# An adaLN block with a gated scan and an FP4 feed-forward: the first stage's opening rewritten, with the input projection's weights laid out by input features

## The chip, the cores and the metric

The kernel runs on one core of a Trainium2 chip. The metric is the device time of one execution in microseconds. TensorE (PE in the profile) multiplies matrices, VectorE (DVE), ScalarE (ACT) and GpSimd (POOL) work elementwise, and SyncE (SP) issues most DMAs. [...]

## The reference, cut to what matters

The input x has 2 sequences of 4096 tokens with 512 features. Six modulation rows per sequence come from a small matrix product. Then follow two residual branches: a gated linear recurrence, and a feed-forward network whose operands are rounded to a 4-bit grid in blocks of 16.

```python
mod = (silu(c) @ wmod).reshape(2, 6, 1, -1)
sa, ca, ga, sb, cb, gb = (mod[:, n] for n in range(6))
ga, gb = floor_of_size(ga, 0.25), floor_of_size(gb, 0.25)      # sign kept
h = layernorm(x) * (1 + ca) + sa
xn = h / norm(h) * sqrt(512) * gamma
q, kv, a = split(xn @ W_qkva.T, 3)
y = scan(y_t = sigmoid(a_t) * y_(t-1) + kv_t)
x = x + ga * (q * y)
h = layernorm(x) * (1 + cb) + sb
x = x + gb * fp4_linear(silu(fp4_linear(h, w_gate)) * fp4_linear(h, w_up), w_down)
```

## The kernel before, in words

The kernel has two stages, each under an order written out by hand: the order of the program is the order in every engine's queue.

**Stage A** computes the recurrence and, beside it, quantizes the feed-forward weights. It goes over 16 blocks of 512 tokens and, in each, over 4 groups `e` of 128 output features: 64 slots. In a slot `mix` (from line 394 on, matmul at L407) makes three products (a, kv, q) of 128 features by 512 tokens, 12 matmuls each. Every operand is split into a high and a low f16 half, and three passes (high-high, high-low, low-high) over 4 pieces of 128 input features make the 12. In the first slot alone the matmuls are cut into pieces of 128 tokens, so that each can start when its 128 tokens have come. Six PSUM banks take the products, three for even and three for odd slots. `gates` (ScalarE sigmoid, L419), `scan` (VectorE, L425) and `read_out` (L434) follow; `halves` (L441) splits the result for a transpose by DMA (L443), `joined` (L449) puts it back together, and `residual` adds it to x on GpSimd (L457) and stores it (L459).

The tokens of a later block are prepared tile by tile (128 tokens): load (L350), moments (L153, L158), reciprocal deviation on GpSimd (L160, L161), `center` and `shift` on VectorE (L166, L172), square sum (L368), gain (L373, L375), high half (L381), low half (L386), and a DMA transpose into `xT` (L390). In the loop each slot prepares one tile, for the block after the current one.

W_qkva stands in memory by output features. So in the **opening** each of its 12 pieces of 128 x 512 is loaded (L208), multiplied with gamma along its columns (L295), squared and summed along its row (L299), scaled by a reciprocal row norm (L302, L303), cut into halves (L322 or L324, and L330) and transposed by DMA into `wqT` (L338). The three gains per group (L310, L313) put the norm back later. `start()` gives this for three of the groups; the fourth is worked off in the first two slots of the loop.

The modulation: `mod_spread` (L221) multiplies the scale and shift rows into all 128 partitions at once for the first sequence (ca, sa); `mod_rows` (L238) makes two rows for both sequences, which `mod_store` (L277) sends to memory for later; `mod_columns` (L252) makes the gate ga by columns in the first slot.

SP issues the loads and the transposes in one queue. A DMA waits until the eighth one before it in that queue has landed.

**Stage B** begins after slot 63, at L902: for each of 64 tiles of 128 tokens the gate and up products (L902), the quantization of the hidden row, and the down product (L949). The change does not touch it.

Of the kernel before, what the change touches and what calls it, by code (L numbers as in the profile page):

```python
# [6 lines left out]

# [10 lines left out]
P = 128  # L18
# [25 lines left out]
def tile_adaln_block(  # L44
# [106 lines left out]
    def moments(xt):  # L151
        st = small.tile([P, 6], F32, name="st", tag="st")
        V.bn_stats(st, xt)  # L153
        return st

    def mean_rstd(st):
        mv = small.tile([P, 2], F32, name="mv", tag="mv", bufs=5)
        V.bn_aggr(mv, st)  # L158
        rstd = small.tile([P, 1], F32, name="rstd", tag="rstd", bufs=5)
        G.tensor_scalar(rstd, mv[:, 1:2], 1e-5, None, ALU.add)  # L160
        G.tensor_tensor(rstd, rstd, mhalf[:, 0:1], ALU.pow)  # L161
        return mv[:, 0:1], rstd
# [32 lines left out]
    wq = {divmod(n, 3): piece(2, n, 1) if n < 11 else piece(1, 2 * KC, 1) for n in range(12)}  # L195
# [3 lines left out]
    with nc.allow_non_contiguous_dma(reason="c is 4 KB"):  # L199
        for b in range(B):  # L200
            S.dma_start(cT[:, :, b], c[b].rearrange("(k p) -> p k", p=P))
    warm = atile([P, 4], F32, "warm")
    A.activation(warm, mhalf, AF.Sigmoid)
    A.activation(sc, cT, AF.Sigmoid)
    V.tensor_mul(sc, sc, cT)

    def load_part(e, part):
        S.dma_start(wq[e, part], w_qkva[part * D + e * P : part * D + (e + 1) * P, :])  # L208

    def load_mod(s, pieces=1):  # L210
        w = KC // pieces
        for k in range(0, KC, w):
            S.dma_start(
                wm[s][:, k : k + w, :],
                wmod[k * P : (k + w) * P, s * D : (s + 1) * D].rearrange("(k p) e -> p k e", p=P),
            )

    def mod_spread(s, b):
        pm = side((P, D))
        for k in range(KC):  # L220
            T.matmul(  # L221
                pm,
                sc[:, k, b : b + 1].to_broadcast([P, P]),
                wm[s][:, k, :],
                start=k == 0,
                stop=k == KC - 1,
            )
        return pm

    def mod_rows(*mods, one_by_one=False):  # L230

        pm = side((P, D))
        rows = [(s, slice(32 * n, 32 * n + B)) for n, s in enumerate(mods)]
        steps = [(k, *r) for k in range(KC) for r in rows]
        if one_by_one:
            steps = [(k, *r) for r in rows for k in range(KC)]
        for k, s, at in steps:
            T.matmul(  # L238
                pm[at, :],
                sc[:, k, :],  # L240
                wm[s][:, k, :],
                start=k == 0,
                stop=k == KC - 1,
                tile_position=(0, at.start),
            )
        return pm, rows

    def mod_columns(s):
        pm = side((P, KC, B))
        for e in range(KC):  # L250
            for k in range(KC):
                T.matmul(  # L252
                    pm[:, e, :],
                    wm[s][:, k, e * P : (e + 1) * P],
                    sc[:, k, :],
                    start=k == 0,
                    stop=k == KC - 1,
                )
        return pm

# [7 lines left out]

    def mod_store(pm, rows):
        row = apool.tile([P, D], F32, name="row", tag="row", bufs=1)  # L270
        for s, at in rows:
            if s == 5:
                mag = apool.tile([P, D], F32, name="mag", tag="y", bufs=3)
                signed_floor(row[at, :], pm[at, :], mag[at, :])
            else:
                A.activation(row[at, :], pm[at, :], AF.Copy, bias=1.0 if s in (1, 4) else 0.0)
            G.dma_start(modd[s], row[at, :])  # L277
# [6 lines left out]
    gam = ctile([P, D], F32, "gam", tag="mod_gb")  # L284
    wqT = atile([P, 2 * KC, 3 * D], F16, "wqT")
    us = atile([P, KC, 3], F32, "us")
    rs = atile([P, KC, 3], F32, "rs")
    gq = atile([P, KC, B], F32, "gq")

    def load_qkva(e):  # L290
        for part in (2, 1, 0):
            load_part(e, part)

    def gamma_qkva(e, part, engine=G):
        engine.tensor_tensor(wq[e, part], wq[e, part], gam, ALU.mult)  # L295

    def square_qkva(e, part):
        sq = work.tile([P, D], BF16, name="sq", tag="sq", bufs=1)
        A.activation(sq, wq[e, part], AF.Square, accum_out=us[:, e, part : part + 1])  # L299

    def inverse_qkva(e, a=0, b=3):
        V.tensor_scalar(rs[:, e, a:b], us[:, e, a:b], 1e-36, 2.0**-28, ALU.max, ALU.mult)  # L302
        G.tensor_tensor(rs[:, e, a:b], rs[:, e, a:b], mhalf[:, : b - a], ALU.pow)  # L303

    def scale_qkva(e):
        inverse_qkva(e)
        gain_qkva(e)

    def gain_qkva(e):
        V.tensor_scalar(  # L310
            us[:, e, :], us[:, e, :], 1e-36, 2.0**-28 / (XGAIN * XGAIN), ALU.max, ALU.mult
        )
        G.tensor_tensor(us[:, e, :], us[:, e, :], phalf[:, :3], ALU.pow)  # L313

    whl = {}

    def hi_qkva(e, part, on_act):
        w = wq[e, part]
        hl = whl[e, part] = new_hl()
        rsc = rs[:, e, part : part + 1]  # L320
        if on_act:
            A.activation(hl[:, 0, :], w, AF.Copy, scale=rsc)  # L322
        else:
            V.tensor_scalar(hl[:, 0, :], w, rsc, None, ALU.mult)  # L324

    def lo_qkva(e, part):
        w = wq[e, part]
        hl = whl.pop((e, part))
        r = part * KC + e
        V.scalar_tensor_tensor(  # L330
            out=hl[:, 1, :],
            in0=w,
            scalar=rs[:, e, part : part + 1],
            in1=hl[:, 0, :],
            op0=ALU.mult,
            op1=ALU.subtract,
        )
        S.dma_start_transpose(wqT[:, :, r * P : (r + 1) * P], flat(hl))  # L338
# [15 lines left out]

    def norm_stats(g):
        xstat[g] = mean_rstd(xstat[g])
# [7 lines left out]
    def norm_square(g):  # L364
        h = xh[g]
        sq = work.tile([P, D], BF16, name="sq", tag="sq", bufs=1)
        ss = small.tile([P, 1], F32, name="ss", tag="ss")
# [3 lines left out]
    def norm_gain(g, engine=V):  # L371
        h, ss = xh[g]
        engine.tensor_scalar(ss, ss, 1e-24, 1.0 / (D * XGAIN * XGAIN), ALU.max, ALU.mult)  # L373
        rn = small.tile([P, 1], F32, name="rn", tag="rn")
# [9 lines left out]
    def norm_lo(g, xT):  # L384
        h, rn, hl = xh.pop(g)
        V.scalar_tensor_tensor(  # L386
            out=hl[:, 1, :], in0=h, scalar=rn, in1=hl[:, 0, :], op0=ALU.mult, op1=ALU.subtract
        )
        t = g % KC
        S.dma_start_transpose(xT[:, :, t * P : (t + 1) * P], flat(hl))  # L390
# [7 lines left out]
    def mix(i, xT, e):  # L398
        ps = [bank(3 * (e % 2) + j) for j in range(3)]
        width = P if i == 0 and e == 0 else TB  # L400
        for t in range(0, TB, width):
            for pp, part in zip(ps, PARTS):
                r = part * KC + e
                n = 0
                for k in range(KC):
                    for wp, xp in PASSES:
                        T.matmul(  # L407
                            pp[:, t : t + width],
                            wqT[:, wp * KC + k, r * P : (r + 1) * P],
# [5 lines left out]
        return i, e, ps  # L415
# [6 lines left out]
    def scan(i, e, ps, sig):  # L422
        y = apool.tile([P, TB], F32, name="y", tag="y", bufs=3)
        init = 0.0 if i % BPB == 0 else carry[e]
        V.tensor_tensor_scan(out=y, data0=sig, data1=ps[1], initial=init, op0=ALU.mult, op1=ALU.add)  # L425
        if i % BPB != BPB - 1:
# [3 lines left out]
        return i, e, ps, y  # L430
# [8 lines left out]
    def halves(i, e, y):  # L439
        yh = apool.tile([P, 2, TB], U16, name="yh", tag="yh", bufs=1)  # L440
        A.copy(yh, y.bitcast(U16).rearrange("p (t h) -> p h t", h=2))  # L441
        yt = apool.tile([P, 2, KC, P], U16, name="yt", tag="yt", bufs=2)
# [12 lines left out]
    def residual(i, e, y):  # L455
        xs = xrows[i][:, :, e * P : (e + 1) * P]
        G.tensor_tensor(xs, xs, y.rearrange("p (t e) -> p t e", t=KC), ALU.add)  # L457
        b, t0 = divmod(i * TB, N)
# [136 lines left out]
    def stats_x(x1):  # L595
# [7 lines left out]
        rstd = small.tile([P, 1], F32, name="rstd", tag="rstd", bufs=5)  # L603
# [57 lines left out]
    def start():  # L661
        a, b_, c_ = PARTS

        def load_mod_piece(s, k):
            S.dma_start(wm[s][:, k, :], wmod[k * P : (k + 1) * P, s * D : (s + 1) * D])

        load_mod(1, KC)
        norm_load(0)
        S.dma_start(gam, gamma.partition_broadcast(P))
        for k, then in enumerate((PARTS[0], PARTS[1], PARTS[2], None)):  # L670
            if then is None:
                norm_load(1)
            else:
                load_part(0, then)
            load_mod_piece(0, k)
        norm_load(2)
        norm_load(3)
        load_qkva(1)
        norm_load(KC)
        pc = mod_spread(1, 0)  # L680
        ps = mod_spread(0, 0)
        pair = mod_rows(1, 0, one_by_one=True)

        norm_moments(0)
        norm_stats(0)
        gamma_qkva(0, a, V)
        A.activation(ca[0], pc, AF.Copy, bias=1.0)
        square_qkva(0, a)
        gamma_qkva(0, b_, V)
        square_qkva(0, b_)  # L690
        inverse_qkva(0, a, a + 1)
        norm_center(0)
        gamma_qkva(0, c_, V)
        inverse_qkva(0, b_, b_ + 1)
        hi_qkva(0, a, True)
        square_qkva(0, c_)
        lo_qkva(0, a)
        inverse_qkva(0, c_, c_ + 1)
        hi_qkva(0, b_, True)
        norm_moments(1)  # L700
        norm_stats(1)
        lo_qkva(0, b_)
        A.copy(sa[0], ps)
        norm_center(1)
        hi_qkva(0, c_, True)
        norm_shift(0)
        norm_square(0)
        lo_qkva(0, c_)
# [366 lines left out]
```

## Time and profile before

| | us |
|---|---|
| median of 3 runs | 1926.46 |
| lowest, highest | 1925.21, 1926.94 |
| the profiled execution | 1928.68 |
| its span, first to last instruction | 1926.9 |
| first matmul of the mix, block 0 | 25.68 |
| first matmul of block 1 (slot 4) | 77.70 |
| first matmul of stage B | 551.11 |

The span of a profile is what lies between the first and the last instruction; the execution's own time has 1.8 us more. The profile names an instruction by the line that issues it, so a helper that several steps call has one line. "Idle before" in a timeline is the time in which the engine had nothing to run, and after the arrow stands what ended it. PEclk is the share of the full TensorE clock that was granted.

### The profile page before, as it was taken

The numbers are of one execution on the slowest core, as the hardware profiler recorded it, in microseconds if no ns is written. First come the engines' busy times: TensorE is split into PE (matmuls) and PEld (weight loads), VectorE is DVE, ScalarE is ACT, GpSimd is POOL, SyncE is SP. The second block draws the span as 40 slices with busy tenths as digits, with TensorE's granted clock in tenths as the row PEclk, the third lists the DMA queues.
The fourth block names the chain that finished last, engine by engine and source line by source line (L and its number), as shares of the span: only waits on it lengthen the run. The fifth ranks groups of instructions, "written<-read, shape, count | busy, mean of one in ns | idle before, by whom it ended". The sixth has DMA issues, their size and how long they took to land.

```text
span 1926.9 us, 25653 instructions
## 1 busy us (share of the span) xinstructions
PE 1897.6 (98%) x9220; PEld 898.6 (47%) x9220; DVE 1604.6 (83%) x2677; ACT 997.3 (52%) x1705; POOL 413.7 (21%) x597
## 2 busy tenths in 40 slices
PE   7899999999999999999999999999999999999998
PEld 4344444444444444444444444444444444444444
DVE  6778889999869988888888888878888888888865
ACT  4555567777755544544454444444444444444432
POOL 4545566566421100000000000001000000000000
PEclk9999999999999999999999999999999999999999
DMA  9797788998733344334433443344334334433333
GB/s 232 174 261 180 177 192 201 224 200 197 170 83 71 76 84 74 64 66 81 75 63 67 80 74 74 68 79 80 63 70 80 72 63 71 81 70 63 64 67 58
DMA packets 483201, 206.67 MB, mean 107 GB/s; under 512 B 439622, under 2 KB 440902, under 8 KB 483072
## 3 DMA queue, kind: packets, MB, share of 16 engines
q1 hardware_dynamic: 468624, 171.50, 41.7%
q0 software_dynamic: 14448, 33.52, 9.6%
q8 instruction: 72, 1.18, 0.3%
q14 instruction: 57, 0.47, 0.1%
HBM read 63.12 MB, written 33.58 MB: 50 GB/s over the span
## 4 chain that ended last, share of the span: by engine, by line
PE 92%; DVE 3%; DMA 1%; ACT 1%; issue 1%; POOL 1%; SPq 0%; ACTq 0%; POOLq 0%; DVEq 0%
PE mm L902 46%; PE sd L949 24%; PE mm L407 22%; DMA scratch<-in_L_attn_W_qkva_dram 1%; DMA xT<-hl 1%; DVE hl L330 0%; POOL xr L457 0%; DVE y L434 0%; DVE ld L172 0%; POOL rs L303 0%; ACT sq L299 0%; DVE xn L122 0%; PE sd L238 0%; ACT yh L441 0%; DVE hl L324 0%
## 5 line engine op out<-in xcount | busy, mean ns | idle before, releaser
L902 PEld LDWEIGHTS <-x2T 128*128 128x128 f16 x4608 | 450.9, 98 | 470.6 <-issue 2.5
L407 PE MATMUL mm<-xT,wqT 128*128 128x512 f16 (+1 forms) x2412 | 506.1, 373 | 15.6 <-DMA xT<-hl 11.3
L902 PE MATMUL mm<-wuT,x2T 128*128 128x512 f16 (+1 forms) x2304 | 487.7, 361 | 2.2 <-DVE hid L922 2.2
L902 PE MATMUL mm<-wgT,x2T 128*128 128x512 f16 (+1 forms) x2304 | 487.7, 361 | 0.0
L949 PE MATMUL sd<-wdT,hT 128*128 128x512 f16 x2112 | 465.8, 379 | 0.0
L407 PEld LDWEIGHTS <-wqT 128*128 128x128 f16 x2412 | 232.4, 99 | 290.1 <-issue 21.6
L949 PEld LDWEIGHTS <-hT 128*128 128x128 f16 x2112 | 206.7, 98 | 242.6
L917 ACT ACTIVATE silu<-mm,u 128x512 f32<-128x512 f32 (+1 forms) x192 | 125.1, 652 | 285.9 <-PE mm L902 282.1
L922 DVE SCALAR_TENSOR_TENSOR hid<-mm,u,silu 128x512 f32<-128x512 f32 (+1 forms) x192 | 128.4, 672 | 140.9 <-PE mm L902 130.7
L604 POOL TENSOR_SCALAR rstd<-vs 128x1 f32<-128x1 f32 x64 | 14.5, 226 | 990.5 <-ACT sq L602 990.5
L143 ACT ACTIVATE u<-ud,rms 128x1 f32<-128x1 f32 x64 | 19.0, 297 | 277.9 <-DVE rms L139 277.9
L120 ACT ACTIVATE sle<-sl 128x512 f16<-128x512 f32 (+2 forms) x162 | 147.2, 909 | 0.0
L113 ACT ACTIVATE she<-sh 128x1408 bf16<-128x1408 bf16 (+1 forms) x128 | 128.5, 1004 | 4.0
L441 ACT COPY yh<-y 128x1024 uint16<-128x1024 uint16 x64 | 67.0, 1047 | 94.7 <-DVE y L434 80.6
L973 POOL DMA_DIRECT2D out_dram<-o x63 | 56.2, 893 | 269.8 <-DVE o L967 266.0
L122 DVE SCALAR_TENSOR_TENSOR xn<-hid,xn 128x1408 f32<-128x1408 f32 x64 | 103.5, 1618 | 3.7 <-ACT hid L116 3.7
L106 DVE TENSOR_TENSOR xn<-hid,inv 128x1408 f32<-128x1408 f32 x64 | 104.0, 1625 | 2.2
L125 DVE SCALAR_TENSOR_TENSOR hhl<-hid,xn 128x1408 f16<-128x1408 f32 x64 | 104.0, 1625 | 2.2
L147 DVE TENSOR_REDUCE amh<-hid 128x88 f32<-128x1408 f32 x64 | 103.7, 1620 | 2.2
L116 ACT ACTIVATE hid<-xn 128x1408 f32<-128x1408 f32 x64 | 88.3, 1380 | 30.7 <-DVE xn L106 30.7
L122 DVE SCALAR_TENSOR_TENSOR xn<-ld,xn 128x512 f32<-128x512 f32 (+1 forms) x98 | 67.0, 683 | 28.9 <-ACT ld L116 28.7
L457 POOL TENSOR_TENSOR xr<-xr,y 128x512 f32<-128x512 f32 x64 | 81.6, 1274 | 19.7 <-ACT y L449 16.1
(113 smaller groups left out, 1907.2 us busy)
## 6 DMA issues: line engine op xcount, KB each, us to landing
ld<-out_dram SPq DMA_DIRECT2D x65, 256.0 KB, 2.9
xr<-in_L_attn_x_dram SPq DMA_DIRECT2D x64, 256.0 KB, 3.5
out_dram<-xr POOLq DMA_DIRECT2D x64, 256.0 KB, 4.1
out_dram<-o POOLq DMA_DIRECT2D x63, 256.0 KB, 3.9
ld<-in_L_ffn_w_gate_dram SPq DMA_DIRECT2D x22, 256.0 KB, 3.3
ld<-in_L_ffn_w_up_dram SPq DMA_DIRECT2D x22, 256.0 KB, 3.4
ld<-in_L_ffn_w_down_dram SPq DMA_DIRECT2D x16, 256.0 KB, 3.3
scratch<-in_L_wmod_dram SPq DMA_DIRECT2D x12, 256.0 KB, 4.7
```

The lines of the kernel that those rows point to most:

```text
L106: V.tensor_tensor(blocks(xn), blocks(src), spread(inv, nb), ALU.mult)
L113: A.activation(blocks(she), spread(sh, nb), AF.Copy, scale=WPEAK)
L116: A.activation(a, xn, AF.Abs, scale=MAGIC)
L120: A.activation(blocks(sle), spread(sl, nb), AF.Copy, scale=WPEAK)
L122: V.scalar_tensor_tensor(out=xn, in0=a, scalar=FLOOR, in1=xn, op0=ALU.max, op1=ALU.add)
L125: V.scalar_tensor_tensor(out=nq, in0=a, scalar=FLOOR, in1=xn, op0=ALU.max, op1=ALU.subtract)
L147: V.tensor_reduce(am, src.rearrange("p (b k) -> p b k", k=QB), AX.X, ALU.max, apply_absolute_value=True)
L407: T.matmul(pp[:, t : t + width], wqT[:, wp * KC + k, r * P : (r + 1) * P], xT[:, xp * KC + k, t : t + width], start=n == 0, stop=n == 3 * ...
L902: T.matmul(pp[:, : n1 - n0], x2T[:, xp * KC + k, :], wt[:, wp * KC + k, n0:n1], start=n == 0, stop=n == 3 * KC - 1,)
L917: A.activation(sl[:, :w], pairs[j][0][:, :w], AF.Silu, scale=u[:, 0:1])
L922: V.scalar_tensor_tensor(out=hid[:, n0:n1], in0=pairs[j][1][:, : n1 - n0], scalar=u[:, 1:2], in1=sl[:, : n1 - n0], op0=ALU.mult, op1=ALU.mult,
L949: T.matmul(pd, hT[:, hp * IC + k, :], wdT[:, wd_chunk(wp, k), :], start=n == 0, stop=n == 3 * IC - 1,)
```

## The change

W_qkva, c and gamma are now laid out by the host before the launch: W_qkva by input features (group, 128 input features, 4 pieces, 3 parts x 128 output features), c and gamma with 128 input features along the partitions. The weights therefore arrive in the orientation in which TensorE needs them, and the DMA transposes of the weights fall away. The rest of the opening follows from it:

- gamma is now a scalar per partition. Squares (`square_qkva`) take it as ScalarE's scale. The norms are sums over partitions, so TensorE makes them with a column of ones (`sum_qkva`); `clamp_qkva` and `power_qkva` turn them into reciprocal roots, rounded to bf16.
- The reciprocal roots lie along partitions and are needed along columns: `diag_qkva` multiplies them with an identity on GpSimd and `spread_qkva` multiplies that with ones on TensorE. `scale_qkva` on VectorE multiplies weights, gamma and these in one operation. `hi_qkva` (ScalarE) and `lo_qkva` (VectorE for groups 0 and 1, GpSimd for groups 2 and 3) cut the halves straight into `wqT`. The gain is the reciprocal of what was used (`gain_qkva`).
- The gate row of both sequences is made together with the two other rows (`rows` of modulations 2, 1, 0), and turned into columns by four small matmuls against a 2 x 2 identity; `mod_columns` is gone.
- TensorE is given 72 and later 36 matmuls of ones with ones (`warm_up`), whose result nobody reads.
- The whole opening, with block 0 and the preparation of tiles up to number 9, is a list of about 300 named steps in a fixed order, `OPENING`. The loop starts at slot 4. In it the order of the steps is the old one; `scan`, `halves` and `residual` are only cut in two.
- Some small pools have more buffers (moments and statistics 10, gains 8).

```diff
-    wq = {divmod(n, 3): piece(2, n, 1) if n < 11 else piece(1, 2 * KC, 1) for n in range(12)}
+    wq = [group(e) for e in range(KC)]
...
-    def gamma_qkva(e, part, engine=G):
-        engine.tensor_tensor(wq[e, part], wq[e, part], gam, ALU.mult)
...
+    def square_qkva(e, k):
+        A.activation(wsq[:, k, :], wq[e][:, k, :], AF.Square, scale=gT[:, k : k + 1])
+
+    def sum_qkva(e, ps):
+        for part in range(3):
+            for k in range(KC):
+                T.matmul(
+                    ps[:, part : part + 1],
+                    wsq[:, k, part * P : (part + 1) * P],
+                    ones[:, :1],
+                    start=k == 0,
+                    stop=k == KC - 1,
+                )
+        return ps
...
+    def power_qkva(e):
+        G.tensor_tensor(rs[:, e, :], us[:, e, :], mhalf[:, :3], ALU.pow)
+
+    def diag_qkva(e):
+        G.tensor_tensor(
+            diag,
+            ident.unsqueeze(1).to_broadcast([P, 3, P]),
+            rs[:, e, :].unsqueeze(2).to_broadcast([P, 3, P]),
+            ALU.mult,
+        )
...
+    def spread_qkva(e, ps):
+        T.matmul(ps, ones, diag.rearrange("p a f -> p (a f)"), start=True, stop=True)
+        return ps
+
+    def scale_qkva(e, k, ps):
+        w = wq[e][:, k, :]
         V.scalar_tensor_tensor(
-            out=hl[:, 1, :],
...
+            out=w, in0=w, scalar=gT[:, k : k + 1], in1=ps, op0=ALU.mult, op1=ALU.mult
+        )
...
-        S.dma_start_transpose(wqT[:, :, r * P : (r + 1) * P], flat(hl))
+    def hi_qkva(e, k):
+        hi, _ = parts_qkva(e, k, 2)
+        A.copy(hi, wq[e][:, k : k + 2, :])
+
+    def lo_qkva(e, k):
+        engine, w = (G, 1) if e > 1 else (V, 2)
+        hi, lo = parts_qkva(e, k, w)
+        engine.tensor_tensor(lo, wq[e][:, k : k + w, :], hi, ALU.subtract)
...
+    OPENING = """
+    warm0 wl0_0 c gT wl0_1 xl_3 xl_0 wm1_0 xl_1 wm1_1 sg sq0_1 wm1_2 mu wm1_3 sq0_0 wm0_0
+    sq0_3 wm0_1 sq0_2 wm0_2 mo_3 wm0_3 sum0 xl_2 cl0 wm2_2 pw0 mo_0 xl_8 wm2_0 rc0 dg0 ms1_0
+    ag_0 ag_3 wm2_1 wm2_3 rs_3 mo_1 sp0 wl1_0 wl1_1 sc0_0 rs_0 ms1_1 xl_5 ag_1 sc0_1 wl2_0
+    rs_1 ms1_2 sc0_3 hi0_0 sc0_2 ms1_3 lo0_0 hi0_1 ms0_0 ca lo0_2 ms0_1 ce_0 ce_3 ms0_2 ce_1
+    ms0_3 warm1 sa mo_2 sh_3 ag_2 xq_3 sh_0 rs_2 sh_1 xq_0 xg_3 mo_8 xq_1 xg_0 ce_2 xg_1
+    xh_0 ag_8 sh_2 rows rs_8 xh_1 xo_0 xq_2 ce_8 xt_0 sq1_1 xg_2 xo_1 sq1_0 wl2_1 sh_8 sq1_3
+    xt_1 sq1_2 mo_5 rst2 sum1 xl_6 xh_2 cl1 rtr ag_5 pw1 mm0_0 gqa xo_2 xq_8 dg1 rc1 xt_2
+    gqf xh_3 xg_8 sq2_0 xo_3 sp1 wl3_0 sq2_1 rs_5 mm0_1 sc1_3 xt_3 sq2_2 sc1_1 sq2_3 sc1_2
+    rst0 wl3_1 pg_1 xl_10 sum2 hi1_1 rdm0 sc1_0 xl_7 mm0_2 cl2 rst1 xl_9 mo_6 pw2 xl_4 hi1_0
+    pg_0 rdm1 ag_6 rc2 lo1_2 mm0_3 sq3_1 dg2 sq3_0 lo1_0 rs_6 ce_5 sp2 ga_0 mm1_0 sc2_1
+    sq3_2 sc2_0 sq3_3 sn_0 hi2_0 lo2_1 sc2_2 sum3 ga_1 mm1_1 cl3 sc2_3 cy_0 pw3 ce_6 hi2_1
+    dg3 rc3 ro_0 lo2_3 pg_3 yh_0 sp3 sh_6 mm1_2 lo2_0 sh_5 xq_6 yt_0 sc3_2 xq_5 lo2_2 sc3_3
+    mo_7 xg_6 hi3_1 mm2_0 mo_4 xg_5 xh_6 ag_7 sc3_0 jo_0 rs_7 ag_4 sc3_1 rs_4 mo_9 mm2_1
+    hi3_0 lo3_3 sn_1 xh_5 lo3_2 ag_9 cy_1 ce_4 ga_2 lo3_1 mm2_2 ro_1 ce_7 lo3_0 yh_1 sh_4
+    rs_9 yt_1 sh_7 xq_4 mm3_0 xo_6 xq_7 xg_4 xo_5 xt_6 xg_7 xh_4 pg_2 re_0 xo_4 xh_7 xt_5
+    mm3_1 xo_7 od_0 xt_4 sn_2 xt_7 cy_2 mm3_2 ro_2 yh_2 yt_2
+    """
...
+        def warm_up(n):
+            pp = bank(2)
+            for _ in range(n):
+                T.matmul(pp[:, :P], ones, ones, start=True, stop=True)
...
-        for slot in range(NS + 3):
+        xT, nxT = new_xT(), new_xT()
+        gate, joining = opening(xT, nxT)
+        for slot in range(KC, NS + 3):
...
+        if name == "L0_attn_W_qkva":
+            a = a.reshape(3, KC, P, KC, P).transpose(1, 4, 3, 0, 2).reshape(KC, P, KC, 3 * P)
```

In the list `wl`, `xl` and `wm` are loads of weights, tokens and modulation weights, `sq sum cl pw dg sp sc hi lo rc` the steps of a weight group, `mo ag rs ce sh xq xg xh xo xt` those of a tile of tokens, `ms` the spread modulation, `rows rst rdm rtr gqa gqf` the rows and the gate, `mm0_q` the 36 matmuls of 128 tokens of slot 0, `mm1_q` to `mm3_q` the 12 matmuls of one product of slots 1 to 3, and `ga sn cy ro yh yt jo re od` what follows them.

## The prediction

> **What bounds the kernel now.** I read the page's busy shares first, then the chain of waits, then the timeline of TensorE alone, because the chain puts nine tenths of the span on one engine.
>
> ```profile
> PE 1897.6 (98%) x9220; PEld 898.6 (47%) x9220; DVE 1604.6 (83%) x2677; ACT 997.3 (52%) x1705; POOL 413.7 (21%) x597
> ...
> PE 92%; DVE 3%; DMA 1%; ACT 1%; issue 1%; POOL 1%; SPq 0%; ACTq 0%; POOLq 0%; DVEq 0%
> ```
>
> The kernel is TensorE's queue of matmuls. A change can gain only where that queue is not running, or runs slowly. TensorE's timeline shows where:
>
> ```profile
> 17.42 5.32 PE L238 MATMUL sd<-scratch,sc 128*2 128x512 f32 x16
> 25.68 2.17 PE L407 MATMUL mm<-xT,wqT 128*128 128x128 f16 x36 [2.94 <-DMA xT<-hl]
> 28.57 2.17 PE L407 MATMUL mm<-xT,wqT 128*128 128x128 f16 x36 [0.72 <-DMA xT<-hl]
> 33.92 5.80 PE L407 MATMUL mm<-xT,wqT 128*128 128x128 f16 x72 [3.18 <-DMA xT<-hl]
> 39.56 3.69 PE L252 MATMUL sd<-sc,scratch 128*128 128x2 f32 x32
> 43.10 17.39 PE L407 MATMUL mm<-xT,wqT 128*128 128x512 f16 x72
> 64.45 9.63 PE L407 MATMUL mm<-xT,wqT 128*128 128x512 f16 x36 [3.96 <-DMA wqT<-hl]
> 77.70 32.49 PE L407 MATMUL mm<-xT,wqT 128*128 128x512 f16 x142 [3.62 <-DMA xT<-hl]
> ...
> 177.65 373.62 PE L407 MATMUL mm<-xT,wqT 128*128 128x512 f16 x1728 [0.24 <-issue]
> ```
>
> Two things are to be seen. First, the opening: block 0 of the first stage (four slots, 36 matmuls each of which slot 0 is cut in 128-column pieces) starts at 25.68 us and the next block only at 77.70. In between lie waits for transposes (3.18, 3.96, 3.62 us) and 3.69 us of tiny column matmuls. Second, the pace: the last line gives 373.62 / 1728 = 0.2162 us per 512-column matmul, so a slot is 36 x 0.2162 = 7.78 us; the two slots at 43.10 should take 15.57 and take 17.39, the one at 64.45 takes 9.63. They run after pauses, at a lower clock. The windows after the opening say how little is left there (columns: length, busy per engine with counts, PEclk, DMA share, GB/s):
>
> ```profile
> 77.70:110.63 32.93, 32.93 (x144) 14.36 (x144) 22.86 (x42) 17.20 (x29) 17.32 (x25) 0.95 0.92 247
> 110.63:111.43 0.80, 0.00 (x0) 0.00 (x1) 0.77 (x2) 0.21 (x2) 0.80 (x1) 1.00 1.28 265
> 143.00:551.10 408.10, 407.76 (x1888) 184.27 (x1887) 364.99 (x697) 286.06 (x511) 232.84 (x307) 1.00 0.82 188
> ```
>
> From 77.70 to stage B at 551.11 are 473.4 us; 60 slots x 7.78 = 467.0 plus 3.6 for the modulation rows make 470.6. So 2.8 us are lost there: 1.8 to clock (32.93 against 31.13 for slots 4 to 7), 0.8 to one transpose, 0.24. Everything after is untouched and TensorE-bound. So the question is one number: when does slot 4 start? Call it T; now T = 77.70.
>
> [...]weight loads go by at 0.43 us each at 45 us and later at 0.216. [...]the trace has 1.27 us for 512 elements[...]:
>
> ```profile
> L457 POOL TENSOR_TENSOR xr<-xr,y 128x512 f32<-128x512 f32 x64 | 81.6, 1274 | 19.7 <-ACT y L449 16.1
> ```
>
> [...]
>
> **The change, part by part.**
>
> *Gone.* 12 weight transposes: each keeps SP's queue 1.23 us or more and the line's landings are 2.7/4.2/7.1 us (min/median/max); three of them back to back land 0.9 us apart. 12 gamma products (0.685 us) and 12 low halves (0.75) and 7 high halves (0.48) on VectorE: 20.6 us. 12 squares with accumulator (0.82) and 5 high halves (0.72) on ScalarE: 13.4. On TensorE 5.32 us of rows one by one, 3.69 of columns, both in the way of block 0. The broadcast load of gamma (256 KB) becomes 2 KB.
>
> *Added.* VectorE: 16 scalings of 384 columns read from PSUM; 512 columns take 0.73 (L434), so 0.60[...]. ScalarE: 16 squares of 384 (0.6) and 8 high halves of 768 (0.85, from 1.05 for 1024 elements at L441): 16.4, so 3 more. GpSimd: 8 low halves of 384 and 4 diagonals of 384, each 1.0 (1.27 scaled[...]); 4 powers of 0.9 replace 11 older ones: about 6 more. TensorE: four column sums (12 weight loads with one column, 0.06 to 0.1 each, I take 0.84 a group), four spreads (0.2), the rows of three modulations (3.6, as the x24 group at 134.85), four little products (1.0), 72 + 36 warming matmuls. The first 72 run from about 1.3 to 7 us, while the loads are still coming; the 36 (2.3 us) stand between the shift's spread and the rows, whose last weights land at about 18.7, so they delay the rows by 1 us at most and sum 1 waits far longer: no cost.
>
> *Up to the first mix.* SP's order is W group 0 and x tiles ahead of the modulation weights. Only eight loads are in flight, each next one waits for the eighth before it, and the queue gives 256 KB per 0.64 us:
>
> ```profile
> 13.05 1.67 SPq L208 DMA_DIRECT2D scratch<-in_L_attn_W_qkva_dram  x3
> ```
>
> Now the last of the shift's weights is in at 16.3 us (its matmul starts at 16.36 on it); the new order has nearly the same bytes ahead of it, less gamma: about 15. Group 0's W at 4.5 and 6.4. Squares end 7.6, sum 8.5, clamp, power, diagonal 10.8 on GpSimd, spread 11.1. VectorE from 11.3: four scalings 2.4, [...]four centers or moments of x 2.9, three shifts 2.25, small ones 0.4 = 9.9, so the third shift is out at 21.2 (sa, at 0.9 per warm spread matmul, is there at 18.2, not late). ScalarE squares to 22.1; GpSimd's scalars (1.05 per tile) 24.3; high halves to 25.0; first transpose issued 24.8, landed 2.7 later at 27.5. But TensorE has group 1's sum and the gate's columns queued ahead of mix 0: ScalarE first does x tile 2 (0.82), four squares (2.4) and the gate row: sum 1 can start at 28.3. That is 3.5 to 5 us after the rows, so the clock is down: 0.84 + 1.0 cost 1.8 more. First mix matmul: about 32. This is 6 us **later** than now (25.68).
>
> *From there.* TensorE's list to slot 4 is 4 x 2.17 + 9 x 12 x 0.2162 + two sums 1.7 + three spreads 0.6 = 34.3 us. Against 52 now. What could interrupt: transposes of x, due 2.7 us after VectorE's low half, all issued before the mixes reach them (30, 34, 37.6 against 34.3, 37.3, 39.5; the last three with under 3 us to spare); weights of groups 2 and 3, whose lows are on GpSimd. There I count from its power of group 2 at about 37.8 to the last low of group 3: two powers (0.9), three deviations (1.45), two gains (1.05), a row send (0.65), two diagonals and eight lows (1.0) = 18.9 us busy in 22, out at 59.7, while the mix of slot 3 could begin at 58.5: 1.2 lost. x transposes 4 to 7 land about 67.7, the end of slot 3 is 67.5. **T = 67.7**. The bounds: GpSimd's pows at their shortest (0.57 + 0.24) give 65.4; 0.06 us more on each instruction gives 71.5.
>
> *After T.* No cold clock (1.8 back). The stall of 0.8 for the transpose of block 2 stays or grows: in slots 5 to 7 each has a 1 MB load besides its 1 MB of other traffic and the DMA engines are at share 1.0 and more, so that transpose (landed 6.95 us after issue) is timed by the queue and not by TensorE; a faster TensorE waits for it, I take 1.2. Net 1.8 - 0.4 = 1.4 gained. VectorE there is at 70%, so it follows.
>
> *Sum.* (77.7 - 67.7) + 1.4 = 11.4 off. The profiled execution has a span of 1926.9 (1928.7 with what lies around it); the median of the runs shown is 1926.5, about the span. Forecast 1926.5 - 11.4 = **1915**.
>
> **Rivals.**
> (B) GpSimd decides. A low half at 1.5 us (f32 and f16 in, f16 out; no such row exists) uses up the 3 us of slack and moves the last low by about 7: T = 74, time 1921.5. For it: L161's one-element power takes 0.57 to 1.54 us, so this engine is uneven; against it: L457 never went over 1.45 in 64 times.
> (C) The small GpSimd steps are short, as at 10 and 21 us in the timeline: T = 65.4, time 1912.5.
> (D) The DMA queue gives it back: with slots 4 to 8 starting closer together, the transposes of blocks 2 and 3 wait for loads, 3 to 4 us in all: 1919. For it: share 1.28 in the stall's window; against it: only one stall of 0.8 now.
> (E) Slower than before: B's mechanism further on. Ten operations of 384 elements are in that chain, so each microsecond on one adds about ten; from 2.1 us each T passes 79, past the break-even of 77.7 + 1.4; at 2.5 T = 84 and the time 1931. [...]L457 shows no such doubling.
> That the change does not do what it says: the instruction order has no weight transposes left and the listed steps in place, so no chance is kept for it.
>
> **Numbers.** Chances: forecast 0.62 (own range 1910.5 to 1919.5), B 0.13, C 0.10, D 0.08, E 0.07. A range of 1909.5 to 1922.5 leaves out E, a part of B and of the tails. What a measurement of this kernel can tell from no change is about 0.2%, 3.9 us: faster than 1922.6 are the forecast, C, D and two thirds of B: 0.89; within: 0.04; slower: 0.07.
>
> **What would show it.** First 128-column mix matmul at 30 to 33 us, slot 4 at 66 to 71; no pause over 1.5 us between; PEclk 0.95 or more from 35 us on; GpSimd's low halves near 1.0 us; slot 8 waiting 0.5 to 2 us for its transpose; stage B at about 540 and 1376 us long as now. Wrong would be: a GpSimd row of 384 elements over 1.5 us, a sum of group 1 after 33 us, a wait for x tiles in block 0, or stalls of more than 2 us between slots 5 and 12.

## The result, and the profile after

| us | before | after |
|---|---|---|
| median | 1926.03 | 1920.32 |
| lowest, highest (8 runs each) | 1925.21, 1927.66 | 1918.39, 1921.61 |
| profiled execution, its span | 1928.68, 1926.9 | 1919.44, 1917.7 |
| first matmul of the mix | 25.68 | 29.64 |
| first matmul of slot 4 (T) | 77.70 | 68.44 |
| from T to stage B | 473.41 | 474.99 |
| from stage B to the end of the span | 1375.8 | 1374.3 |

The ratio of the times is 0.9968, with a 95% interval of 0.9957 to 0.9979: the kernel is 4 to 8 us faster, by the medians 5.7. The forecast was 11.4.

The page's busy shares and its chain, by engine, for the kernel after:

```profile
PE 1897.7 (99%) x9364; PEld 904.6 (47%) x9364; DVE 1603.0 (84%) x2666; ACT 998.9 (52%) x1702; POOL 419.1 (22%) x604
...
PE 94%; DVE 2%; DMA 1%; POOL 1%; issue 1%; ACT 0%; SPq 0%; DVEq 0%; POOLq 0%
```

TensorE is busy for as long as before (1897.6) although it has 144 matmuls more; the gain is idle time. TensorE's timeline of the same execution (start, duration, line, operation, count, idle before and what ended it):

```profile
1.11 6.71 PE L757 MATMUL mm<-scratch 128*128 128x128 bf16 x72 [1.11 <-DVE scratch L217]
...
26.36 0.20 PE L300 MATMUL mm<-scratch,scratch 128*128 128x1 bf16 x2 [4.19 <-ACT scratch L295]
27.38 0.43 PE L300 MATMUL mm<-scratch,scratch 128*128 128x1 bf16 x10 [0.81 <-ACT scratch L295]
27.85 1.86 PE L735 MATMUL sd<-id,row 2*128 2x2 f32 x8
29.64 4.02 PE L430 MATMUL mm<-xT,wqT 128*128 128x128 f16 x36
...
33.76 2.17 PE L430 MATMUL mm<-xT,wqT 128*128 128x128 f16 x36
...
58.10 7.51 PE L430 MATMUL mm<-xT,wqT 128*128 128x512 f16 x34 [1.06 <-POOL wqT L348]
68.44 32.63 PE L430 MATMUL mm<-xT,wqT 128*128 128x512 f16 x144 [2.83 <-DMA xT<-hl]
103.89 23.48 PE L430 MATMUL mm<-xT,wqT 128*128 128x512 f16 x108 [2.82 <-DMA xT<-hl]
...
356.95 186.64 PE L430 MATMUL mm<-xT,wqT 128*128 128x512 f16 x864 [0.61 <-DMA xT<-hl]
```

The reader is to see five places. The first piece of the mix takes 4.02 us where the next takes 2.17: it comes after a pause of 4.19 us ahead of the sum of group 1 and runs cold, that is, at half the TensorE clock (PEclk 0.50 from 29.64 to 33.50). Slot 3 waits 1.06 us for GpSimd's low half. Then come three waits for transposes of x: 2.83 ahead of slot 4, 2.82 ahead of slot 8 (block 2), 0.61 ahead of block 10. Before, these three were 3.62, 0.80 and none. The windows around them (length, busy time and count for PE, PEld, DVE, ACT and POOL, then PEclk, DMA share, GB/s):

```profile
65.61:68.44 2.83, 0.00 (x1) 0.03 (x2) 1.05 (x2) 2.02 (x3) 0.00 (x0) 0.90 0.72 171
68.44:101.07 32.63, 32.63 (x144) 14.32 (x144) 23.89 (x43) 18.16 (x30) 17.58 (x25) 0.96 0.89 254
101.07:103.89 2.82, 0.00 (x1) 0.01 (x1) 2.30 (x5) 0.20 (x2) 1.74 (x3) 1.00 1.25 135
```

In the pause ahead of slot 8 the DMA share is 1.25: the DMA engines are at work and TensorE has nothing to do. What led to the pause ahead of slot 4 is in the chain of work over that stretch (start, duration, what):

```profile
53.60 4.44 POOL wqT L348 x4
58.04 0.64 POOL rstd L164
...
58.75 0.93 POOL rstd L165
...
60.09 0.94 POOL rn L392
...
62.01 0.73 ACT hl L398
...
62.80 1.36 issue
...
64.27 3.92 DMA xT<-hl
```

GpSimd's four last low halves hold up the scalars of the last x tile, these the high half, and the transpose issued at 64.27 lands only 3.92 us later. The 1.36 us of "issue" are the low half of that tile on VectorE:

```profile
62.77 1.48 DVE L403 SCALAR_TENSOR_TENSOR hl<-ld,rn,hl 128x512 f16<-128x512 f32 x1 [0.20 <-ACT hl L398]
```

The one before it, at 61.82, takes 0.75 us. Both run beside GpSimd's residual of slot 0 (L485, from 61.95), which takes 1.75 us there and 1.26 in slot 1.

### The profile page after: what moved, and what is told of

It reads as the page before. It is cut to its first block, busy times and chain, and to the rows that moved or that the text cites. A ratio compares the mean times of both kernels' runs of the same rounds, so it can differ in the third digit from the quotient of the medians.

```text
span 1917.7 us, 25880 instructions
## 1 busy us (share of the span) xinstructions
PE 1897.7 (99%) x9364; PEld 904.6 (47%) x9364; DVE 1603.0 (84%) x2666; ACT 998.9 (52%) x1702; POOL 419.1 (22%) x604
## 4 chain that ended last, share of the span: by engine, by line
PE 94%; DVE 2%; DMA 1%; POOL 1%; issue 1%; ACT 0%; SPq 0%; DVEq 0%; POOLq 0%
PE mm L946 47%; PE sd L993 24%; PE mm L430 23%; DMA xT<-hl 1%; PE mm L757 0%; DMA xr<-in_L_attn_x_dram 0%; PE sd L230 0%; DVE ld L176 0%; DVE scratch L334 0%; POOL wqT L348 0%; DVE y L448 0%; POOL rn L392 0%; PE sd L244 0%; DVE hl L403 0%; POOL rstd L165 0%
## 5 line engine op out<-in xcount | busy, mean ns | idle before, releaser
L966 DVE SCALAR_TENSOR_TENSOR hid<-mm,u,silu 128x512 f32<-128x512 f32 (+1 forms) x192 | 128.4, 672 | 138.9 <-PE mm L946 130.3
L485 POOL TENSOR_TENSOR xr<-xr,y 128x512 f32<-128x512 f32 x64 | 82.0, 1281 | 20.8 <-ACT y L477 17.4
```

The lines of the kernel that those rows point to most:

```text
L966: V.scalar_tensor_tensor(out=hid[:, n0:n1], in0=pairs[j][1][:, : n1 - n0], scalar=u[:, 1:2], in1=sl[:, : n1 - n0], op0=ALU.mult, op1=ALU.mult,
```

## The experiments

The theory after the result: **(1)** the opening does what was forecast, and about 9 us of it are real; **(2)** the clock that the forecast gave back after slot 4 was a chance of the one execution that I read; **(3)** the waits after slot 4 are new, belong to this kernel, and come from the DMA queue. The rivals: the profile of after is the chance one, or GpSimd or the missing weight transposes do something that I had not priced.

**A second profile of each kernel.** No edit.

> The kernel before, unchanged, profiled once more, to see which stretches vary from one execution to the next. Theory 1 (the profile of before that the prediction used was a long execution by a wait that comes and goes): slot 4 again at 77.7 within 0.5 us, stage B again at 551 within 1, and the 2.2 us wait for VectorE's hid product at the start of stage B shorter or gone, span 1924 to 1925. Theory 2 (the opening itself varies): slot 4 moves by more than 1 us, and stage B with it.

> The changed kernel, unchanged, profiled once more. If the waits before slot 4 and before slot 8 (2.8 us each in the first profile) belong to the kernel, both come again within 0.7 us, slot 4 at 68.4 within 0.7 and stage B at 543.4 within 1.5. If they are chance, one of them is under 1.5 us.

TensorE's timeline of the kernel before, second execution:

```profile
77.17 31.24 PE L407 MATMUL mm<-xT,wqT 128*128 128x512 f16 x144 [3.06 <-DMA xT<-hl]
109.32 23.48 PE L407 MATMUL mm<-xT,wqT 128*128 128x512 f16 x108 [0.91 <-DMA xT<-hl]
...
581.43 2.75 PE L902 MATMUL mm<-wuT,x2T 128*128 128x512 f16 x12 [1.68 <-DVE hid L922]
```

and of the kernel after, second execution:

```profile
67.75 31.24 PE L430 MATMUL mm<-xT,wqT 128*128 128x512 f16 x144 [2.82 <-DMA xT<-hl]
102.03 23.48 PE L430 MATMUL mm<-xT,wqT 128*128 128x512 f16 x108 [3.05 <-DMA xT<-hl]
...
355.99 186.64 PE L430 MATMUL mm<-xT,wqT 128*128 128x512 f16 x864 [1.49 <-DMA xT<-hl]
...
574.29 2.75 PE L946 MATMUL mm<-wuT,x2T 128*128 128x512 f16 x12 [0.56 <-DVE hid L966]
```

The kernel before runs slots 4 to 7 in 31.24 us this time, at the full clock (granted 1.00), where the forecast's execution took 32.93. So the 1.7 us of clock that the forecast wanted back come and go with the execution: a third execution with the same opening, the kernel before with its loads spread (below), loses them again (granted 0.53 in its first 3.55 us of slot 4). T differs by 9.42 us here and by 9.26 in the first pair. The wait ahead of slot 8 is 0.91 against 3.05 (0.80 against 2.82): it repeats, and so does that ahead of block 10 (1.49 at 355.99 in this execution of after, none before). From T to stage B the change now loses 474.71 - 471.31 = 3.4 us. Behind stage B it gains 1.1, because the one wait there, for the hidden row (L922 before, L966 after), falls from 1.68 to 0.56. Sum: 9.4 - 3.4 + 1.1 = 7.1 us, within the interval of the ratio. For the kernel before, neither expectation came out whole: slot 4 is at 77.17, but stage B begins at 548.48, 2.6 us earlier, and what varied is the clock behind slot 4, which neither named. For the kernel after both waits came again. The clock behind the wait ahead of slot 4 did not: these are the windows of the first 3.5 us of slot 4, in the first profile of after and in the second (columns as above).

```profile
68.44:72.00 3.56, 3.56 (x11) 1.33 (x12) 3.54 (x6) 2.41 (x4) 2.44 (x3) 0.60 0.54 150
67.75:71.30 3.55, 3.55 (x17) 1.66 (x18) 3.52 (x6) 2.72 (x5) 2.45 (x3) 1.00 0.55 151
```

**Spreading the modulation loads.** In slots 5 to 7 the kernel loads three matrices of 1 MB, whole. Cut into twelve loads of 256 KB, in slots 5 to 16:

```diff
-    MODS = 10
+    MODS = 18
...
-            if MODS - 5 <= slot < MODS - 2:
-                load_mod(slot - MODS + 8)
+            if 5 <= slot < 17:
+                s_, k_ = divmod(slot - 5, KC)
+                load_mod(3 + s_, k_, k_ + 1)
```

> The changed kernel, but the loads of the last three modulation matrices, 1 MB each in slots 5, 6 and 7, are cut into twelve of 256 KB over slots 5 to 16, and the rows made from them come in slot 18 instead of 10. Theory Q (the three large loads fill the DMA queue in front of block 2's last transpose): the wait before slot 8 falls from 2.8 to under 0.7 us, nothing as large takes its place, time about 2 to 2.5 us less than the changed kernel, 1918. Theory P (the transposes are late because of the traffic of a slot as a whole and VectorE's pace): the wait is over 1.5 us or comes back before slot 12 or 16, time within 0.7 us of the changed kernel, 1920.3.

The queue of SyncE in the kernel after, ahead of slot 8 (start, time of the issue, operation):

```profile
92.25 0.57 SPq L224 DMA_DIRECT2D scratch<-in_L_wmod_dram  x1
92.86 0.50 SPq L503 DMA_DIRECT2D ld<-in_L_ffn_w_gate_dram  x1
93.48 0.36 SPq L503 DMA_DIRECT2D ld<-in_L_ffn_w_up_dram  x1
93.89 0.54 SPq L360 DMA_DIRECT2D xr<-in_L_attn_x_dram  x1
94.88 2.52 SPq L409 DMA_TRANSPOSE xT<-hl  x1
```

The modulation load of 1 MB, three loads of 256 KB, and then the transpose that slot 8 needs. That an issue in this queue waits for the eighth before it to land is in the profile of before: the nine issues from 8.57 to 15.01 us begin 0.02 us after that landing, none of the 531 issues behind the first eight begins ahead of it, and the loads of 256 KB land 0.62 to 0.70 us apart there. The answer on that tile alone, from 90 to 104 us, gives the time from its issue to its landing:

```profile
DMA to landing us min/median/max: 9.0/9.0/9.0
```

and the timeline of TensorE with the loads spread:

```profile
68.77 118.40 PE L430 MATMUL mm<-xT,wqT 128*128 128x512 f16 x540 [2.73 <-DMA xT<-hl]
```

Slots 4 to 18 run in one piece: the wait ahead of slot 8 is gone, and the two transposes of x issued between 91 and 104 us, that of slot 8 (95.51) among them, land 4.3 to 5.8 us after their issue instead of 9.0. Two smaller waits, 0.47 and 1.30 us ahead of blocks 9 and 10, stand in place of the one ahead of block 10. The time is 1918.5 (ratio 0.9962, 0.995 to 0.9975). By the medians that is 1.8 us less than after, though the two intervals overlap; the place is shown by the trace. This execution has a cold clock behind its wait of 2.73 us (granted 0.52 in the 3.53 us after it): the same 540 matmuls take 116.71 us in the last run of this section.

**The same on the kernel before**, to see whether the change made this queue dearer.

> The kernel before, with the loads of the last three modulation matrices cut into twelve and spread over slots 5 to 16, as in mods_spread. Theory Q (the opening that ends 9 us earlier moved slots 5 to 8 against this queue, so that the change itself made the queue dearer): here only the wait of 0.8 to 0.9 us ahead of slot 8 goes, and the time falls by 0.5 to 1.0 us against the kernel before, less than the 1.8 us that the same edit gave on the changed kernel. Rival (the queue costs both kernels the same, and the change has nothing to do with it): the time falls by 1.8 us or more.

1925.62 us (ratio 0.9997, 0.9989 to 1.0005): 0.5 us less than the 1926.11 of its comparison, not separable from nothing, nor quite from 1.8. The timeline:

```profile
77.45 118.40 PE L407 MATMUL mm<-xT,wqT 128*128 128x512 f16 x540 [3.73 <-DMA xT<-hl]
```

The wait ahead of slot 8 is gone here too. There were 0.9 us to gain, against 3.05 in the kernel after. By the traces theory Q stands; the times alone would not decide it.

**Without the warm-up.** `warm0` and `warm1` struck from the list:

```diff
-    warm0 wl0_0 c gT wl0_1 xl_3 xl_0 wm1_0 xl_1 wm1_1 sg sq0_1 wm1_2 mu wm1_3 sq0_0 wm0_0
+    wl0_0 c gT wl0_1 xl_3 xl_0 wm1_0 xl_1 wm1_1 sg sq0_1 wm1_2 mu wm1_3 sq0_0 wm0_0
...
-    ms0_3 warm1 sa mo_2 sh_3 ag_2 xq_3 sh_0 rs_2 sh_1 xq_0 xg_3 mo_8 xq_1 xg_0 ce_2 xg_1
+    ms0_3 sa mo_2 sh_3 ag_2 xq_3 sh_0 rs_2 sh_1 xq_0 xg_3 mo_8 xq_1 xg_0 ce_2 xg_1
```

> The changed kernel without its 108 warming matmuls, nothing else moved. Theory N (they stand in idle time and their clock is lost again in the pause before the sum of group 1): ca and sa at most 1 us later, slot 4 within 1 us of 68.4, time within 0.7 us of 1920.3. Theory W (they carry the opening): the column sum and the eight spread products run at half clock, 0.5 us for the sum and 0.85 more per product until the clock comes, sa 2 to 3.5 us later and with it the transposes of x and the first mix; slot 4 at 70.5 to 72, time 2 to 3.5 us more, 1922.5 to 1924.

```profile
9.18 2.05 PE L230 MATMUL sd<-scratch,sc 128*128 128x512 f32 x2 [0.40 <-DMA scratch<-in_L_wmod_dram]
...
70.40 32.78 PE L430 MATMUL mm<-xT,wqT 128*128 128x512 f16 x144 [3.11 <-DMA xT<-hl]
```

The first modulation products of TensorE's timeline take 2.05 us instead of 1.10, the sum of group 1 starts at 27.64 instead of 26.36, and T is 70.40. Time 1921.76 (ratio 0.9982, 0.9973 to 0.999), 1.4 us more than after by the medians. The two intervals overlap a little, but T is 2.0 and 2.7 us later than in the two profiles of after. So the warm-up, which the forecast put at no cost and no gain, is worth about 1.4 us: theory W's way, with T just under its range and the time under it.

**Filling the pause.** 56 more warming matmuls in the 4.19 us ahead of the sum of group 1:

```diff
-            warm=lambda n: warm_up((72, 36)[n]),
+            warm=lambda n: warm_up((72, 36, 56)[n]),
...
-    xh_0 ag_8 sh_2 rows rs_8 xh_1 xo_0 xq_2 ce_8 xt_0 sq1_1 xg_2 xo_1 sq1_0 wl2_1 sh_8 sq1_3
+    xh_0 ag_8 sh_2 rows warm2 rs_8 xh_1 xo_0 xq_2 ce_8 xt_0 sq1_1 xg_2 xo_1 sq1_0 wl2_1 sh_8 sq1_3
```

> The changed kernel with 56 more warming matmuls behind the modulation rows, in the 4.2 us pause of TensorE before the sum of group 1. Theory C (the pause takes the clock, so the first mix piece runs at half speed, 4.02 us instead of 2.17, and everything behind it in the queue, group 1's spread above all, is late by that): the first piece takes 2.2 us, group 1's spread comes 1.5 to 2 us earlier, slot 4 at 66.5 to 67.2, time 1 to 1.8 us less than 1920.3. Theory L (what follows waits for VectorE and GpSimd anyway): the first piece is faster, and slot 4 moves by less than 0.5 us.

```profile
22.45 3.30 PE L757 MATMUL mm<-scratch 128*128 128x128 bf16 x56
26.71 0.20 PE L300 MATMUL mm<-scratch,scratch 128*128 128x1 bf16 x2 [0.96 <-ACT scratch L295]
27.73 0.40 PE L300 MATMUL mm<-scratch,scratch 128*128 128x1 bf16 x10 [0.81 <-ACT scratch L295]
28.20 1.05 PE L735 MATMUL sd<-id,row 2*128 2x2 f32 x8
29.18 3.78 PE L430 MATMUL mm<-xT,wqT 128*128 128x128 f16 x36
```

The pause in this timeline of TensorE is 0.96 instead of 4.19 us and the small products for the gate take 1.05 instead of 1.86, but the first piece of the mix still takes 3.78 (4.02), and the next one 2.17. Theory C's fast first piece did not come. T is 67.56, 0.9 us earlier than in the first profile of after but only 0.2 earlier than in the second, and the wait ahead of slot 8 is 1.73 in this execution. Time 1918.37 (ratio 0.9954, 0.9941 to 0.9966): about 2 us less than after by the medians, with overlapping intervals. What the edit gives through the opening is thus 0.2 to 0.9 us; where the rest comes from is not shown.

**The last transposes ahead of the store.** The transposes of tiles 4 to 7 stand behind GpSimd's residual and store of slot 0 (and the deviation of tile 9). These three steps moved behind them:

```diff
-    rs_9 yt_1 sh_7 xq_4 mm3_0 xo_6 xq_7 xg_4 xo_5 xt_6 xg_7 xh_4 pg_2 re_0 xo_4 xh_7 xt_5
-    mm3_1 xo_7 od_0 xt_4 sn_2 xt_7 cy_2 mm3_2 ro_2 yh_2 yt_2
+    yt_1 sh_7 xq_4 mm3_0 xo_6 xq_7 xg_4 xo_5 xt_6 xg_7 xh_4 pg_2 xo_4 xh_7 xt_5
+    mm3_1 xo_7 xt_4 sn_2 xt_7 rs_9 re_0 od_0 cy_2 mm3_2 ro_2 yh_2 yt_2
```

> The changed kernel with three steps at the end of the list put later: the deviation of tile 9, the residual of slot 0 and its store now stand behind the transpose of tile 7. Theory S (the store of 256 KB stands in the DMA queue in front of the last transpose of block 1, and GpSimd's steps delay its gains): that transpose lands 2.75 us after its issue instead of 3.9, slot 4 starts 1.2 to 1.8 us earlier, 66.3 to 67.2, with a wait of about 1.3 instead of 2.8; time 0.8 to 1.8 us less than 1920.3. Rival (SP issues four transposes in 5.6 us, and the last is bound by that or by VectorE): slot 4 moves by less than 0.5 us.

```profile
67.44 31.24 PE L430 MATMUL mm<-xT,wqT 128*128 128x512 f16 x144 [1.45 <-DMA xT<-hl]
101.87 25.17 PE L430 MATMUL mm<-xT,wqT 128*128 128x512 f16 x108 [3.18 <-DMA xT<-hl]
```

TensorE's wait ahead of slot 4 falls from 2.83 to 1.45, near the 1.3 of theory S; what the store and what GpSimd's steps gave of it is not shown. But the wait ahead of slot 8 is 3.18, and the time is 1919.72 (ratio 0.9963, 0.9949 to 0.9976), 0.6 less than after and not to be told from it. Slot 4 is 1.0 us earlier than in the first profile of after and 0.3 earlier than in the second. Slot 8 starts 0.2 us before where the second profile had it (102.03), after the longer wait: hardly anything of the gain is left there. That the queue holds it back fits, but each figure is of one execution.

**The low halves on VectorE.** The rival that GpSimd's low halves decide:

```diff
-        engine, w = (G, 1) if e > 1 else (V, 2)
+        engine, w = (V, 1) if e > 1 else (V, 2)
```

> The changed kernel with the eight low halves of weight groups 2 and 3 on VectorE instead of GpSimd, in the same places of the list. In the changed kernel they take 0.93 us each on GpSimd (one 1.37), and TensorE waits 1.06 us for the last one. Theory G (GpSimd is the tighter of the two there): the wait goes, slot 4 comes 0.5 to 1 us earlier, 67 to 67.9. Theory V (VectorE, 94% busy between 40 and 66 us, is the tighter): eight times 0.56 = 4.5 us more on it, partly returned[...]; slot 4 at 70 to 72, time 1.5 to 3.5 us more than 1920.3.

T is 69.64, 1.2 and 1.9 us later than in the profiles of after, slot 3 waits 0.96 us for its low half, now VectorE's, and the time is 1920.99 (ratio 0.9971, 0.996 to 0.9982): not to be told from after. Theory G is out, since the wait stays; of theory V the direction of T is there, not its size. Why so little happens is seen best in one line of VectorE, the shifts of x, between 40 and 66 us (duration in ns, minimum, median and maximum; first and last start). After:

```profile
L176 DVE SCALAR_TENSOR_TENSOR ld<-ld,rstd,sa x4: 741/1398/1478, 46.7 to 58.5; 128x512 f32<-128x512 f32 x4
```

With the low halves on VectorE:

```profile
L176 DVE SCALAR_TENSOR_TENSOR ld<-ld,rstd,sa x4: 739/742/745, 47.4 to 59.4; 128x512 f32<-128x512 f32 x4
```

And the windows of the same stretch, after:

```profile
40.00:66.00 26.00, 24.52 (x127) 10.91 (x124) 24.52 (x39) 14.40 (x26) 20.66 (x27) 1.00 0.25 58
```

and with the low halves on VectorE:

```profile
40.00:66.00 26.00, 24.55 (x134) 11.34 (x132) 24.47 (x47) 14.64 (x26) 13.07 (x20) 1.00 0.25 59
```

VectorE took over eight low halves of 0.54 us each, 4.3 us of work, and is busy for 24.47 us of this stretch as for 24.52 before: eight operations more fit into the same time. In the profile of after the three shifts that run beside GpSimd's low halves take 1.40 to 1.48 us each; the fourth, which begins after the last of them, takes 0.74. With the low halves gone from GpSimd, the four shifts take 2.05 us less in all, the four centers (L170) 0.60 and four small products (L608) 0.62. So 3.3 of the 4.3 us come back, and the 1.0 that is left fits a T that is 1.2 us later than in the first profile.

**The three edits together** (loads spread, pause filled, steps moved):

> The three together: modulation loads spread, the pause filled, the end of the list reordered. If their gains are in different places they add: slot 4 at 65.5 to 66.5, no wait over 1 us before slot 8, time 1915 to 1916.5, under both kernels. If slot 4 is held by one common thing, the time is that of the best single one, 1917.5 to 1918.5.

```profile
29.02 3.16 PE L430 MATMUL mm<-xT,wqT 128*128 128x128 f16 x36
...
66.05 116.71 PE L430 MATMUL mm<-xT,wqT 128*128 128x512 f16 x540 [1.44 <-DMA xT<-hl]
...
350.39 186.64 PE L430 MATMUL mm<-xT,wqT 128*128 128x512 f16 x864 [0.82 <-DMA xT<-hl]
```

1913.51 us (1912.11 to 1915.34), ratio 0.9934 (0.9921 to 0.9946): this version beats both kernels: by 13.1 us the 1926.61 of its comparison, and by 6.8 us the median of after. TensorE's timeline shows T at 66.05 and 536.87 - 66.05 = 470.8 us from there to stage B, with one wait of 0.82 in it, where the forecast counted 470.6 for 60 slots without a stall. The time is below the 1915 to 1916.5 expected, and its interval lies clear of after's. Singly the edits gave 1.8, 2.0 and 0.6 us by the medians. Together they give more than this sum of 4.4, though the excess is not clear of the noise in three such differences. It fits the reading of the run with the steps moved, that an earlier slot 4 pays more once the queue ahead of slot 8 is clear. It also fits the clock: the wait ahead of slot 4, 1.44 us here, takes no clock (540 matmuls in 116.71 us), while the wait of 2.73 in the run with the loads spread cost 1.7 us (118.40). No run here parts the two.

## Why the prediction was right in its direction and in T, and twice too large in its gain

- **First mix matmul at 32: 29.64.** Sum 1 began at 26.36 instead of 28.3; a column sum takes 0.4 to 0.5 us instead of 0.84. The cold clock at this place (granted 0.50 from 26.90 to 33.73) was foreseen, but its price is larger than the 1.8 us charged to the sums and small products: the small products took 1.86 where 1.0 was put, and the first piece of the mix, for which the list had 2.17, took 4.02, 2.7 us more together.
- **GpSimd's low halves 1.0 us each, 1.2 us lost at slot 3: right.** They take 0.91 to 1.37, median 0.93, and slot 3 waits 1.06. The 1.0 was my estimate from the 1.27 us of 512 elements at L457. VectorE's time for its own low halves of 768 elements was an estimate too, and not one from the trace; they took 0.95 in the median (L348). Rivals B and E fall with that row, rival C with T.
- **T = 67.7: 68.44 and 67.75, right, though in part by luck.** TensorE came to the end of slot 3 at 65.61, 1.9 us before the forecast's 67.5, and then stood for 2.83 us. The forecast had the last transpose of x landing at 67.7, which is nearly right (68.19), and gave it 0.2 us of wait only because TensorE was thought to be later. So 1.9 us too early and 2.6 us of wait too much cancel. About 1.4 us of that wait are the place of the store and the residual ahead of the transposes, as the moved steps show.
- **"After T": the step that failed.** The forecast gained 1.4 us there, as "No cold clock (1.8 back)" and a stall of 0.8 that grows to 1.2. In the two pairs of profiles the change loses 1.6 and 3.4 us there. The 1.8 comes and goes: the kernel before runs slots 4 to 7 at the full clock in its second profile, and the kernel after lost 1.39 there in its first, so it could not be counted as a gain of the change. The stall was mis-sized: 2.82 and 3.05 instead of 1.2, plus 0.61 and 1.49 ahead of block 10, for which the sum had no term. This is rival D's mechanism, at about its size of 3 to 4 us, and the run with the loads spread shows the three loads of 1 MB as the cause at slot 8; why block 10 waits is open. I had the sentence for it ("timed by the queue and not by TensorE") and should have drawn its consequence: what the queue times comes less early than TensorE does. T came 9.26 and 9.42 us earlier, slot 8 only 7.54 (from 111.43 to 103.89) and 7.29 (from 109.32 to 102.03), so that about 2 us of the earlier start were waited off there.
- **"Stage B 1376 us long as now": 1.1 to 1.5 us shorter**, through the wait at L966. The sum had no term for it, and no run here says why it is shorter.
- **Base.** The execution that the sum was made against was, at 1928.68, 2.65 us above the median of its kernel. The forecast set that median beside the execution's span, 1926.9, and found them about equal, but a span leaves out 1.8 us. So a term that made this execution long, its cold clock, was taken off a median that need not hold it. By the second pair the terms give 7.1 us; the 1.4 to the medians' 5.7 lies within the interval and stays open.
- **Warm-up at no cost: true as cost, but it left out its gain** of about 1.4 us. Since T came out as forecast, that too was covered by other terms.

Of the marks set beforehand for a wrong forecast, one appeared: a stall of more than 2 us between slots 5 and 12. The mark "no pause over 1.5 us" between the first mix and slot 4 broke too, at its very end.

## What to carry to other kernels

When an opening is shortened, look first at the next place where a transfer is timed by a full queue, and count the loads that stand ahead of it: here about 2 of 9 us of the earlier start were lost there, until those loads were cut up. Before a term such as a cold clock goes into a sum, look at several executions of the same kernel: it may be in some and not in others, before the change and after it. Small edits at both ends of such a stretch are worth trying together, since what one gains can be waited off at the other.

## What the runs showed of the hardware that was not expected

- **Whether a wait was followed by a lower clock did not go by its length.** The waits meant are those over 2 us ahead of slots 4 and 8 and of block 10. After 2.31 and 3.11 us (no warm-up), 2.73 (loads spread), 2.83 (after), 3.18 (steps moved), 3.62 (before) and 3.73 (before with loads spread) the next stretch took 1.4 to 1.7 us more (for instance 32.63 and 32.93 against 31.24, and 25.17 against 23.48). The clock granted in its first 3.5 us was 0.52 (loads spread), 0.53 (before with loads spread), 0.56 (steps moved), 0.59 (before) and 0.60 (after). After 2.24 (no warm-up), 2.54 and 3.24 (low halves on VectorE), 2.75 (pause filled), 2.82 (first profile of after, at slot 8), 2.82 and 3.05 (second profile of after) and 3.06 (second profile of before) nothing was lost. Where the waits lay is seen in the first profile of each kernel. The stretches of stage A at 0.50 begin at 33.94, 44.18, 64.66 and 78.32 us in before and last 3.41 us each; their starts are 10.24, 20.48 and 13.66 us apart, 3, 6 and 4 times 3.41. In after they begin at 26.90 (6.83 us long) and 67.86 (3.41), 40.96 us apart, 12 times 3.41. In the 3.41 us ahead of five of these six TensorE stood idle for 3.18, 3.20, 2.80, 3.21 and 2.25 us; the one at 44.18 is the next point. Two waits of over 2 us behind the first 20 us of stage A of these profiles were not followed by a lower clock: 2.94 us ahead of the first mix in before and 2.82 ahead of slot 8 in after. If steps of 3.41 us are counted from 33.94 and from 67.86, the first is cut at 23.70 into 0.96 and 1.98 us, the second at 101.99 into 0.92 and 1.90. That counting is my estimate from these starts, since the clock does not change at 23.70 or 101.99, and no run moved a wait on purpose to test it.
- **The clock fell behind column products without a pause.** In the kernel before, TensorE is busy throughout from 40.77 to 44.18, most of it with the column products of the gate (128x2), and the clock is 0.50 from 44.18 to 47.60; this is the 17.39 us where the forecast counted 15.57. In the second profile of before the 60 matmuls behind the same products take 13.31 us, 0.34 more than at 0.2162 each, so that it was not lost there. With the pause filled, the first piece of the mix still took 3.16 (three edits together) and 3.78 us instead of 2.17, after a stretch of column sums, small products and two waits of 0.8 to 1.0 us; which of these it was is not shown.
- **Where GpSimd and VectorE ran side by side, VectorE was slowed most.** Beside GpSimd's low halves three shifts took 1.40 to 1.48 us and one center (L170, at 54.64) 1.31, where the others took 0.74. Not all operations there were slower: another center (at 56.53) took 0.74, and the scaling at L334 (at 43.34), which reads PSUM, took 0.58 where the median is 0.60. What decides it is not shown. GpSimd's times vary too: five of its eight low halves took 0.91 to 0.93 and three 1.36 to 1.37, and the residual beside the doubled low half of L403 took 1.75 instead of 1.26. The forecast looked for this on GpSimd's rows, where L457 showed nothing, and not on VectorE's.
